# An attention and deformable-convolution block: five turns per tile moved from TensorE to DRAM blocks and VectorE, row biases moved into accumulating DMAs, orders replanned

## The chip, the cores and the metric

The kernel runs on one core of one Trainium2 chip. The metric is the device time of one execution in microseconds (us). Several executions are timed and their median is given; one more execution is recorded by the hardware profiler, and all busy times, waits and durations come from that one.

The core has TensorE (PE, with its weight loads shown as PEld), VectorE (DVE), ScalarE (ACT), GpSimd (POOL) and SyncE (SP). SP computes nothing here. It issues DMAs, each after the waits that stand ahead of it in SP's own order.

## The reference

Two layers on an image batch `x` of shape (4, 64, 64, 256), all in float32.

```
# layer 0: self-attention over the 4096 pixels of each image
q, k, v = x @ wq + bq, x @ wk + bk, x @ wv + bv          # q, k: 32 channels, v: 256
x = gamma * softmax(q k^T) v + x

# layer 1: deformable convolution (16 groups of 16 channels, 9 points), then an MLP
h      = ln(x) * ln1_g + ln1_b
proj   = h @ inproj_w + inproj_b                         # padded by one pixel
c      = gelu(ln(depthwise3x3(h) + dw_b))
offset = c @ off_w + off_b                               # (x, y) of 16 * 9 points
mask   = softmax over the 9 points of (c @ mask_w + mask_b)
s      = sum over the points of mask * bilinear(proj at the pixel + point + offset)
x      = x + s @ outproj_w + outproj_b
h      = ln(x) * ln2_g + ln2_b
x      = x + gelu(h @ fc1_w + fc1_b) @ fc2_w + fc2_b
```

## The kernel before

The 16384 pixels are cut into 64 tiles of 256 (UN = 64; NU = 16 tiles for each of the 4 images, 128 pixels twice on the partitions). A tile passes through these stages, each a dictionary of named steps:

- `project(b, u)` turns a tile of x, so that its channels lie on the partitions, and makes keys, queries (`keys`, `key_bias`) and values. For image 0 this comes ahead of everything (the stage "first", turned on TensorE). For the images 1 to 3 it is done while the image before is in attention; there x is read in blocks of 32x32 by `in_blocks` (four DMAs of 128-byte pieces, which put each block where its turned form belongs), and one VectorE transpose (`copy`, L645) turns the values inside each block. Keys, queries and values of later images go through DRAM (`kd`, `qd`, `vd`).
- `Attention` makes the energies `e` (L752), their exponentials `ex` on ScalarE (L762) and the weighted sums `acc` (L774), with a column of ones for the softmax's denominator.
- `front` adds the attention's result times gamma to x (`inverse`, `residual`), takes the statistics, normalises (`norm`), turns (`turn`), scales, puts the result into a strip of image rows `hs` (`image`), adds outproj_b to x and stores it as `x1d` (`keep`), and projects it and stores the padded image `xp` (`project_in`, `store`).
- `plan(v)` works on tiles that are shifted by half a tile (65 of them, the first and last half as long): the nine taps of the depthwise convolution on `cv` (L874, L878), a turn (`turn`, tile `pc`, L891), layer norm, a turn back (`turn2`, `pt_p`), gelu, the heads for offsets and masks (`po`, L915), and from these the weights `wn` of a 5x5 window around each pixel.
- `sample(v)` loads five shifted rows of `xp` (`win`, L1074), multiplies them by the weights (`times`, L1094) and adds them up (`plus`, L1102; `across`), giving `sp`.
- `back(v)` (built by `finish`) turns sp (`pt_s`), applies outproj, adds it to x1 (`added`, L1182), layer norm, a turn (`pt_b`), fc1 in eight parts `ph` (L1200), gelu (L1208), fc2 (`pmlp`, L1217), and stores the result (`end`, L1223). `raised` (L1189) adds fc2_b.

So a tile is turned on TensorE five times after the attention: `pt_f`, `pc`, `pt_p`, `pt_s`, `pt_b`. Such a turn is four matmuls against the identity matrix `ident` (`transposed`, L331, for four of the five). It writes PSUM, and ScalarE or VectorE takes it from there. The row biases bv, inproj_b, outproj_b and fc2_b are added by VectorE, each with one operation on 128x512 elements (L681, L838, L824, L1189), from copies that all partitions hold.

Layer norm's `1/sqrt` is done on GpSimd (`rstd`: L289 adds epsilon, L290 takes the power), between VectorE's statistics (`mv`, L287) and VectorE's `nm` (L295), the shift that ScalarE's `norm` needs.

The order in which each engine does its work is written out: the table `WHEN` has a time for every step within a slot of T = 60 units, the table `LATE` has other times for the last slots (from 59 on), and `whole` sorts all steps of all tiles by slot and time. Only the order counts, and each engine follows it. Slot s holds the attention of tile s and, further on in the pipeline, `front`, `plan`, `sample` and `back` of earlier tiles. DMAs take SP's queue in the order of the steps that issue them.

A further part of the program (a loop over `whole(True)`, and rounds for points outside the 5x5 window) runs only if the data ask for it. One such round for far points, `far_round`, is always run at the end.

## Time and profile before

| | |
|---|---|
| median of 3 runs | 3754.59 us (3753.15 to 3758.33) |
| the profiled execution's own time | 3755.45 us |
| its span, first to last instruction | 3753.7 us, mean granted TensorE clock 0.995 |
| PE, PEld | 98%, 85% of the span busy |
| DVE, ACT, POOL | 92%, 57%, 8% busy |
| DMA queue of SP | 51.9% of the 16 engines' span, 508 MB |
| DMA issues of SP with most calls | win<-xp 536, kT<-kd 512, qs<-qd 256, xs<-in_x_dram 192 |

A busy share is an average over the whole run. Matmuls are pipelined, and their recorded durations overlap; the cost of a matmul in a row of them is the distance from its start to the start of the next. The same holds for VectorE's operations, which overlap by some 0.08 us.

### The profile page before, as it was taken

To read this page: it belongs to the slowest core of one execution; us is meant where nothing else is said; L and a number is where in the kernel's file an instruction comes from. 1 tells how busy PE (TensorE), PEld (TensorE's weight loads), DVE (VectorE), ACT (ScalarE), POOL (GpSimd) and SP (SyncE) were. 2 spreads that over 40 slices of the span, in tenths; PEclk is the share of its full clock that TensorE was granted. 3 is DMA by queue.
4 is the path that set the end of the run, shared out by engine and by line. 5 is a ranking of instruction groups with operands and counts; after the bars stand their busy time and mean duration, and the time that the engine had idled before them with its cause. 6 is when DMAs were issued, how large, how long until landed. Compare 5 with 4: busy or idle time off the path is not lost.

```text
span 3753.7 us, 53218 instructions
## 1 busy us (share of the span) xinstructions
PE 3693.6 (98%) x18226; PEld 3185.1 (85%) x18226; DVE 3442.1 (92%) x6307; ACT 2122.0 (57%) x4085; POOL 313.1 (8%) x444
## 2 busy tenths in 40 slices
PE   7999999999999999999999999999999999999988
PEld 6888888888888888888888888888888888888867
DVE  2499999999999999999999999999999999999995
ACT  2465565565565565565565555555565665565543
POOL 1000000000000000000000000000000000000021
PEclk9999999999999999999999999999999999999999
DMA  6555545556555555555656455555565545544531
GB/s 185 142 130 140 143 129 140 141 129 175 149 149 146 138 131 143 134 135 143 176 137 164 129 138 142 129 139 140 138 174 146 136 124 136 132 129 126 135 83 52
DMA packets 370088, 518.42 MB, mean 138 GB/s; under 512 B 144560, under 2 KB 287472, under 8 KB 369808
## 3 DMA queue, kind: packets, MB, share of 16 engines
q1 hardware_dynamic: 359904, 508.02, 51.9%
q10 hardware_dynamic: 8320, 3.43, 0.4%
q8 instruction: 147, 2.41, 0.3%
q0 software_dynamic: 1584, 3.47, 0.3%
q14 instruction: 133, 1.09, 0.1%
HBM read 385.91 MB, written 128.85 MB: 137 GB/s over the span
## 4 chain that ended last, share of the span: by engine, by line
PE 89%; DVE 5%; issue 0%; DMA 0%; ACT 0%; POOL 0%; DVEq 0%; SPq 0%; ACTq 0%; POOLq 0%
PE acc L774 43%; PE pmlp L1217 11%; PE ph L1200 11%; PE e L752 6%; PE po L915 5%; PE pout L1175 3%; PE pp L831 3%; PE pv L670 2%; DVE pw L1094 1%; PE pkq L651 1%; DVE cv L878 1%; DVE pw L1102 1%; PE pt_s L331 1%; PE pt_b L331 1%; PE pt_p L331 1%; PE pc L891 1%
## 5 line engine op out<-in xcount | busy, mean ns | idle before, releaser
L774 PE MATMUL acc<-V,ex 128*128 128x257 f32 x8192 | 1887.0, 380 | 0.0
L774 PEld LDWEIGHTS acc<-V,ex 128*128 128x128 f32 x8192 | 1537.3, 190 | 223.3 <-issue 21.7
L1094 DVE TENSOR_TENSOR pw<-win,wn 128x1280 f32<-128x1280 f32 x640 | 931.5, 1481 | 10.9 <-ACT wn L1038 1.9
L1102 DVE TENSOR_TENSOR pw<-pw,pw 128x1280 f32<-128x1280 f32 x492 | 729.7, 1483 | 0.1
L762 ACT ACTIVATE ex<-e 128x512 f32<-128x512 f32 x1024 | 529.7, 605 | 26.1 <-PE e L752 18.0
L1200 PE MATMUL ph<-hT_b,f1w 128*128 128x256 f32 (+1 forms) x2080 | 487.9, 377 | 5.2 <-ACT gT L1208 2.8
L1217 PE MATMUL pmlp<-f2w,gT 128*128 128x256 f32 x2048 | 462.7, 379 | 1.3 <-DVE x1b L1182 1.1
L1200 PEld LDWEIGHTS ph<-hT_b,f1w 128*128 128x128 f32 x2080 | 378.1, 190 | 67.3 <-ACT gT L1208 6.3
L1217 PEld LDWEIGHTS pmlp<-f2w,gT 128*128 128x128 f32 x2048 | 384.2, 190 | 51.8 <-DVE x1b L1182 1.4
L878 DVE SCALAR_TENSOR_TENSOR cv<-hs,dw,cv 128x256 f32<-128x256 f32 (+1 forms) x1076 | 424.3, 459 | 1.4 <-ACT cv L874 1.3
L303 ACT ACTIVATE xn_p<-pc,nm_p,rstd_p 128x256 f32<-128x256 f32 x128 | 65.4, 561 | 541.1 <-DVE nm_p L295 541.1
L1208 ACT ACTIVATE gT<-ph,f1b 128x256 f32<-128x256 f32 (+1 forms) x520 | 236.6, 468 | 236.1 <-PE ph L1200 234.6
L752 PE MATMUL e<-qs,kT 128*128 128x256 f32 x2048 | 321.7, 300 | 0.0
L752 PEld LDWEIGHTS e<-qs,kT 128*128 128x128 f32 x2048 | 271.4, 190 | 8.1 <-ACT ex L762 0.8
L762 ACT ACT_TABLE_LOAD x182 | 233.5, 1283 | 3.1
L289 POOL TENSOR_SCALAR rstd_p<-mv_p 128x2 f32<-128x2 f32 (+1 forms) x65 | 76.2, 1172 | 1669.1 <-DVE mv_p L287 1597.9
L915 PE MATMUL po<-om_w,ge 128*128 128x432 f32 x512 | 196.5, 526 | 0.8 <-ACT ge L908 0.8
L1004 DVE TENSOR_TENSOR pr<-hat 128x1296 f32<-128x1296 f32 x128 | 192.6, 1505 | 0.0
L1208 ACT ACT_TABLE_LOAD x124 | 159.1, 1283 | 2.2
L915 PEld LDWEIGHTS po<-om_w,ge 128*128 128x128 f32 x512 | 96.9, 190 | 70.5 <-issue 54.7
L908 ACT ACTIVATE ge<-pt_p,bd,gd 128x256 f32<-128x256 f32 (+1 forms) x130 | 66.0, 558 | 137.9 <-PE pt_p L331 137.9
L303 ACT ACTIVATE xn_b<-x1b,nm_b,rstd_b 128x256 f32<-128x256 f32 x128 | 70.0, 593 | 129.8 <-DVE nm_b L295 129.8
(220 smaller groups left out, 3823.0 us busy)
## 6 DMA issues: line engine op xcount, KB each, us to landing
win<-xp SPq DMA_DIRECT2D x536, 320.0 KB, 4.5
kT<-kd SPq DMA_DIRECT2D x512, 256.0 KB, 4.2
omd<-om SPq DMA_DIRECT2D x63, 432.0 KB, 2.6
x<-in_x_dram SPq DMA_DIRECT2D x64, 256.0 KB, 3.0
x1d<-x SPq DMA_DIRECT2D x64, 256.0 KB, 2.2
xp<-xq SPq DMA_DIRECT2D x128, 128.0 KB, 2.4
x1b<-x1d SPq DMA_DIRECT2D x63, 256.0 KB, 3.2
spd<-sp SPq DMA_DIRECT2D x63, 256.0 KB, 2.2
```

Of the source, the lines that this page charges most:

```text
L303: nc.scalar.activation(xn[:, i, :], s, AF.Identity, bias=nm[:, i : i + 1], scale=st["r"][:, i : i + 1])
L752: nc.tensor.matmul(es[r][:, jj, :], lhsT=self.kT[g][:, 4 * jj + r, :], rhs=self.qs.bitcast(F32R), start=True, stop=not self.general,)
L762: nc.scalar.activation(ex, self.es[r], AF.Exp)
L774: nc.tensor.matmul(self.acc[i], lhsT=ex[:, jj, i * P : (i + 1) * P], rhs=V[t // 2][:, t % 2, :], start=(g == 0 and r == 0 and jj == 0), st ...
L878: nc.vector.scalar_tensor_tensor(dst, src, dw[:, k, j : j + 1], dst, ALU.mult, ALU.add)
L915: nc.tensor.matmul(st["po", i], lhsT=st["ge"][:, k, i * P : (i + 1) * P], rhs=om_w[:, k, :], start=(k == 0), stop=(k == 1),)
L1004: nc.vector.tensor_mul(pr.rearrange("p a b c d g -> p a b (c d g)"), hat[:, :, i, 1, :].unsqueeze(1).to_broadcast([P, 3, 3, S]), hat[:, :, ...
L1094: nc.vector.tensor_mul(st[r].rearrange("p d (g c) -> p (d g) c", c=GC), src.rearrange("p d (g c) -> p (d g) c", c=GC), wns[v][:, i, r] .re ...
L1102: nc.vector.tensor_add(st[0], st[0], st[r])
L1200: nc.tensor.matmul(ph[:, :m], lhsT=f1w[:, k, c * P : (c + 1) * P], rhs=st["hT"][:, k, :m], start=(k == 0), stop=(k == 1),)
L1208: nc.scalar.activation(st["gT"][:, c, :m], st["ph", c][:, :m], AF.Gelu, bias=f1b[:, c : c + 1])
L1217: nc.tensor.matmul(po, lhsT=st["gT"][:, c, i * P : (i + 1) * P], rhs=f2w[:, c, :], start=(c == 0), stop=(c == NH - 1),)
```

## The change

The five turns of a tile leave TensorE for most tiles. A tile that is to be turned is written to DRAM by SP (`sent`, into one of four buffers `ways`), read back in blocks of 32x32 by the four DMAs of `in_blocks` (`blocks`), and turned inside the blocks by one VectorE transpose (`swapped`). For sp the copy that was written to DRAM anyway (`spd`) serves. The first tile and the last four to seven keep the turns on TensorE: each stage has a condition of the form `0 < v < UN - 5`. The condition is on the tile's number, UN - 4 for the turn in `front`, UN - 5 for both in `plan`, UN - 6 for both in `back`.

The row biases leave VectorE. ScalarE writes gamma*bv into the tile of x ahead of time (`base`), and x is then added by an accumulating DMA of GpSimd (`input`); the values are scaled by gamma instead. The same is done with outproj_b (`base` and `load` in `back`). SP fills the image `xp` and the output in DRAM with inproj_b and fc2_b (`fill`), and an accumulating DMA of GpSimd adds the tile (`store`). Some VectorE work is merged (two sums, two mask products, two reciprocals), and the inner hat goes to ScalarE.

All orders are new: `WHEN` has other numbers for every stage, and `LATE` now covers the first slots (0 to 4, and the stage "first") and the slots from 55 on. The numbers of both tables are left out below.

```diff
+    ways = dram.tile([4, 256, C], F32, name="ways")
+    turns = [0]
+
+    def blocks(name, src=None, read=None):
+        t = p1.tile([P, 2, 256], F32, tag="xs", bufs=2, name=f"bl_{name}")
+        in_blocks(t, *(read or (src, 0, 2)))
+        return t
+
+    def sent(src):
+        way = ways[turns[0] % 4]
+        turns[0] += 1
+        nc.sync.dma_start(way.rearrange("(q p) c -> p q c", p=P), src)
+        return way
+
+    def swapped(dst, bl):
+        nc.vector.transpose(dst.rearrange("p k t -> p (k t)"), bl.rearrange("p k t -> p (k t)"))
+        return dst
...
-        def value_bias():
-            bias = bv_s.unsqueeze(1).to_broadcast([P, 2, C])
...
-                nc.vector.tensor_add(vs, st["pv"], bias)
+                nc.scalar.activation(vs, st["pv"], AF.Identity, scale=gamma_s)
...
+        def base(self):
             self.x = p2.tile([P, 2, C], F32, tag="x1", name=f"x1_{self.n}")
-            nc.sync.dma_start(self.x, xt_[self.b, self.u])
+            nc.scalar.copy(self.x, gbv.unsqueeze(1).to_broadcast([P, 2, C]))
+
+        def input(self):
+            nc.gpsimd.dma_start(self.x, xt_[self.b, self.u], accum_op=ALU.add)
...
+        through = 0 < b * NU + u < (UN if att.general else UN - 4)
...
             normalised(st, [att.x[:, i, :] for i in range(2)], f"f{n}")
+            if through:
+                st["way"] = sent(st["xn"])
 
         def turn():
-            st["pt"] = transposed(st["xn"], f"f_{n}")
+            if through:
+                st["bl"] = blocks(f"f_{n}", st["way"])
+            else:
+                st["pt"] = transposed(st["xn"], f"f_{n}")
+
+        def swap():
+            st["hT"] = swapped(p3.tile([P, C // P, 256], F32, tag="cT", name=f"hT_f{n}"), st["bl"])
...
+        def fill():
+            nc.sync.dma_start(
+                xp[b, 2 + 4 * u : 6 + 4 * u, 2 : 2 + W, :],
+                bass.AP(inproj_b.tensor, inproj_b.offset, [[0, 4], [0, W], [1, C]]),
+            )
+
+        def take():
+            st["xq"] = p1.tile([P, 2, C], F32, tag="xq", name=f"xq_{n}")
+            nc.scalar.copy(st["xq"], st["pp"])
+
         def store():
-            xq = p1.tile([P, 2, C], F32, tag="xq", name=f"xq_{n}")
-            nc.vector.tensor_add(xq, st["pp"], inb.unsqueeze(1).to_broadcast([P, 2, C]))
             for r in range(2):
-                nc.sync.dma_start(
+                nc.gpsimd.dma_start(
                     xp[b, 2 + 4 * u : 6 + 4 * u, 2 : 2 + W, :].rearrange("(q r) w c -> r w q c", r=2)[r],
-                    xq[r * W : (r + 1) * W, :, :],
+                    st["xq"][r * W : (r + 1) * W, :, :], accum_op=ALU.add,
                 )
...
+        through = 0 < v < (UN if general else UN - 5)
+
         def turn():
+            if through:
+                st["bl"] = blocks(f"c_{n}", sent(st["cv"]))
+                return
...
-            nc.vector.scalar_tensor_tensor(
-                hat[:, 1], hat[:, 0], 1.0, hat[:, 2], ALU.subtract, ALU.subtract, reverse0=True
-            )
+            nc.scalar.activation(hat[:, 1], xy, AF.Abs)
+            nc.scalar.activation(hat[:, 1], hat[:, 1], AF.Identity, bias=every[:, 0:1], scale=-1.0)
...
-    def back(v, sps):
+    def back(v, sps, general):
...
+        def base():
+            st["x1"] = p2.tile([P, 2, C], F32, tag="x1b", name=f"x1b_{v}")[:, :nt]
+            nc.scalar.copy(st["x1"], ob.unsqueeze(1).to_broadcast([P, nt, C]))
+
         def load():
-            st["x1"] = p2.tile([P, 2, C], F32, tag="x1b", name=f"x1b_{v}")[:, :nt]
-            nc.sync.dma_start(st["x1"], x1t_[:, g0 : g0 + nt])
+            nc.gpsimd.dma_start(st["x1"], x1t_[:, g0 : g0 + nt], accum_op=ALU.add)
+
+        def fill():
+            nc.sync.dma_start(
+                outs[g0 * P : (g0 + nt) * P, :],
+                bass.AP(fc2_b.tensor, fc2_b.offset, [[0, nt * P], [1, C]]),
+            )
+
+        def store():
+            nc.gpsimd.dma_start(out_[:, g0 : g0 + nt], st["x1"], accum_op=ALU.add)
```

## The prediction

> **What bounds the kernel now.** I read section 1 of the page and the chain first, then the windows by stage, then the timeline of one steady slot on TensorE and VectorE.
>
> ```profile
> PE 3693.6 (98%) x18226; PEld 3185.1 (85%) x18226; DVE 3442.1 (92%) x6307; ACT 2122.0 (57%) x4085; POOL 313.1 (8%) x444
> PE 89%; DVE 5%; issue 0%; DMA 0%; ACT 0%; POOL 0%; DVEq 0%; SPq 0%; ACTq 0%; POOLq 0%
> ```
>
> ```profile
> 60.00:150.00 90.00, 85.56 (x421) 73.74 (x420) 23.84 (x63) 44.67 (x80) 1.76 (x4) 0.98 0.59 143
> 2000.00:3000.00 1000.00, 1000.00 (x4968) 866.66 (x4967) 957.11 (x1721) 587.57 (x1125) 79.04 (x108) 1.00 0.55 143
> 3500.00:3600.00 100.00, 94.56 (x453) 79.00 (x451) 99.47 (x183) 46.78 (x92) 9.94 (x13) 1.00 0.38 100
> ```
>
> Columns of the windows: stretch, length, busy PE, PEld, DVE, ACT, POOL, granted clock, DMA share, GB/s. From about 150 to 3400 us PE never pauses, so there PE's work is the time; DVE follows at 96%. PE loses 23 us before 150 us and 29 us after 3400 (one window of that stretch is shown). A slot of the loop, read between two turns of sp:
>
> ```profile
> 2001.51 0.60 PE L331 MATMUL pt_s<-ident,sp 128*128 128x128 f32 x4
> 2001.86 1.19 PE L752 MATMUL e<-qs,kT 128*128 128x256 f32 x8
> ...
> 2022.45 0.60 PE L331 MATMUL pt_f<-ident,xn_f 128*128 128x128 f32 x4
> 2022.88 1.90 PE L774 MATMUL acc<-V,ex 128*128 128x257 f32 x8
> ...
> 2057.99 0.60 PE L331 MATMUL pt_s<-ident,sp 128*128 128x128 f32 x4
> ```
>
> From 2001.51 to 2057.99 is 56.48 us. Matmuls overlap, so a turn costs what lies between its start and the next start: 0.35 (pt_s), 0.43 (pt_f), and on the same timeline 0.44 (pc), 0.43 (pt_p), 0.36 (pt_b). In the same slot DVE's pauses are these, 2.54 us in all, so its work is 53.9 us:
>
> ```profile
> 2004.82 0.69 DVE L1182 TENSOR_TENSOR x1b<-x1b,pout 128x512 f32<-128x512 f32 x1 [0.16 <-PE pout L1175]
> 2009.25 0.16 DVE L295 SCALAR_TENSOR_TENSOR nm_b<-mv_b,rstd_b 128x2 f32<-128x2 f32 x1 [0.60 <-POOL rstd_b L290]
> 2011.75 0.17 DVE L797 RECIPROCAL rall<-acc 128x1 f32<-128x1 f32 x1 [0.23 <-PE acc L774]
> 2044.36 0.69 DVE L1223 TENSOR_TENSOR x1b<-x1b,pmlp 128x512 f32<-128x512 f32 x1 [0.85 <-PE pmlp L1217]
> 2053.27 0.61 DVE L924 TENSOR_TENSOR om<-po,om_b 128x432 f32<-128x432 f32 x1 [0.70 <-PE po L915]
> ```
>
> **What the Trainium skill says.** "VectorE: DVE Perf Modes", The three transpose paths: VectorE turns only 32x32 blocks; the placing of the blocks is left to the block reads. The trace has this already for x: one STREAM_TRANSPOSE of 128x512 takes 703 ns. "DMA: Bandwidth & Descriptors", Two DMAs through the same engine are not ordered: a read of what another DMA wrote must wait for the first one's completion. So each turn now pays a whole write and then a read: 2.0 us (vd<-vs) and 2.6 us (xs<-in_x_dram) to landing in this trace. The same page, SWDGE vs HWDGE: accumulation during a DMA can only be issued from GpSimd; no run here shows an accumulating DMA yet. "SBUF — State Buffer", SBUF: two separate sides: a GpSimd op that reads SBUF can be locked out by a running DVE op with two SBUF inputs. The trace agrees: L289 for rstd_p, started beside a 1.48 us pw<-win, has a median of 1291 ns, for rstd_b 327 ns.
>
> **The change part by part, in us per slot of 56.48.**
>
> PE: five turns go, 0.35+0.43+0.44+0.43+0.36 = 2.01. Nothing is added, so PE needs 54.47. By the limits in the code, pt_f goes in 59 slots, pc and pt_p in 58, pt_s and pt_b in 57: 59x0.43 + 58x0.87 + 57x0.71 = 116 us in all. This is the most that the removal can give.
>
> DVE: five block transposes at 0.63 from start to start (703 ns less the 0.08 by which neighbours overlap): +3.14. Removed, in the same measure: f2b 0.60, ob 0.57, inb 0.60, bv 0.60, inner hat 0.61, two products with gamma 0.17, one reciprocal 0.08, and by merging two mask products and two sums 0.07+0.16: -3.46. Net -0.3, so 53.6 of work. In the last batch (slots from 48 on) the bv add is absent anyway, and DVE gains 0.3 of work.
>
> DVE's new waits, from the built order and these durations. (a) After mv_p DVE runs a 1.40 us plus and two 0.10 us bounds before nm_p needs rstd_p. L289 is locked out until the plus ends; then L290 takes 0.71: about 0.7 of wait. (b) On SP the reads for swap of hT_b stand behind the stores of kq, and these wait for kq1 (L659). From there: two issues 0.8, three reads at 0.69, the last landing 2.6: 5.5 us; DVE has 4.6 us of work between. Wait (a) lies in the same stretch, so both together cost about 1.0. Bounds: 0 (SP runs ahead) and 2.5 (each landing 1.5 longer). (c) The pauses for po, pmlp and pout now come at other places; in the order they come after DVE's waits have let PE run ahead, so I take 0, at most the old 1.7. Sum for DVE 54.6, beside PE's 54.5: nearly equal. I take 54.7 a slot. What is late next is then DVE, and PE waits for its block transposes.
>
> ACT: copies of gbv and ob, the scaling of vs and the copy of xq at 0.59 each (the row sT<-pt_s), Abs and Identity at 0.67 each (the row hat<-om), less the copy sT: +3.1 on 33.2. Cover: ACT is idle 23 us per slot. Nothing on the path.
>
> SP: 20 more block reads at 0.69, three sends and two fills at about 0.45; less x, x1b, out and two xp (2.9): +13.2 us of issuing. SP's waits are some 36 us of a slot, so the total fits; the order of its waits decides, as in (b). The two writes of image and result wait for their fills, which stand half a slot ahead of them: 0.
>
> POOL: five accumulating DMAs per slot. Their issue is not in the trace: from 0.59 (xp<-zeros) to 1.45 (indirect f_am), so 3 to 7 us beside 5 of work. Behind a waiting one stand L289 and L290 of rstd_p, and behind these DVE's nm_p. The store of xq is the one just ahead; it waits for ACT's copy of pp, which PE finishes some 2 us before mv_p. I take 0; bounds 0 and 1.5. A gain is excluded, since a wait is only added.
>
> DMA share: 55% now. 289 block reads of 256 KB in 128-byte pieces: 2048 pieces at 13 ns (the mean of such packets in the trace) on 16 engines, 1.66 us each, 13% of the span. Sends (174 of 256 pieces of 1 KB at 58 ns, likewise) 4%, fills 3%; accumulation at between one and three times a plain transfer, 0 to 12%. Sum 75 to 87%. Not the bound, but landings may lengthen; that is the upper end of (b).
>
> Head and tail: all orders of slots 0 to 4 and 55 on are new, and the last turns stay on PE. PE idles 52 us there. I take a gain of 5, bounds +35 (8.3 us pass before the first x lands, and I leave 9 for the last serial steps) and -20.
>
> Sum against the profiled run (3755.45, span 3753.7): slots 2 to 47, 46 x 1.8 = 83; ten slots of the last batch, where PE would fall from 53.9 to 51.9 but DVE with its waits holds at 53.4: 5; ends 5. 3755.45 - 93 = 3662; the median of the runs is 0.9 below the profiled run: 3661, forecast **3660**.
>
> **Rivals.**
> 1. DVE becomes the bound by a clear margin: waits (a), (b) and POOL sum to 2 us rather than 1. The slot is 55.6, the gain 46 x 0.9 = 41, nothing in the last batch: 3710 (3690 to 3745). For it: the balance of 54.6 to 54.5. Against: DVE idles 2.5 us per slot today, and the order puts other work between.
> 2. The way through DRAM is late: a turn takes 0.1 + 2.0 + 0.1 + 3x0.69 + 2.6 = 6.9 us on an SP queue in which a late send also holds back win and kT. Place: SP's sends and reads, waited for by DVE at the block transposes. It decides from about 1.9 us per slot beyond the 1.0 of (b), where the gain of PE is used up. At 3.5 us beyond, the slot is 58: 3755 + 56x1.5 = 3840, **slower**. For it: SP's load grows by two thirds and DMA goes to about 80%. Against: every pair of send and swap that I placed has 8 to 12 us of DVE work between.
> 3. The ends: with the full 116 and 35 at the ends it would be 3755 - 151 = 3604; 20 lost there with the likeliest rest gives 3685.
> 4. The turns don't leave PE (the limits exclude most slots): excluded, since the built order has no turn on PE in the slots between.
>
> **The numbers.** About 0.2% is what a measurement of this kernel can tell from no change: 7.5 us. Likeliest case 0.57, 3660 (3625 to 3690); rival 1 0.22; rival 2 0.14; a result within 0.2% 0.03; ends at their best 0.04. Faster 0.83, same 0.03, slower 0.14. The range from 3600 to 3780 leaves out most of rival 2 and little below.
>
> **What would show it.** Right: PE has no L331 rows in mid-run, is busy 98% or more from 300 to 2900 us, and a slot is 54.5 to 55. Step (a) is right if DVE waits some 0.7 us per slot for POOL's rstd_p; (b) if it waits under 1 us for bl_b. The DMA step is wrong if block reads need over 4 us to land, POOL's if rstd_p waits for xq. The forecast is wrong if PE's busy share falls below 96% in mid-run, with waits for the block transposes (rival 1, then 2).

## The result, and the profile after

The changed kernel takes **4341.91 us** (median of 4 runs, 4330.33 to 4347.3) beside 3754.36 for the kernel before: a ratio of 1.1559 (1.1534 to 1.1584). It is 588 us slower; 3660 was forecast, with 0.14 on slower. Its profiled execution took 4330.33 us (span 4328.4), at a mean TensorE clock of 0.942, where before had 0.995.

Section 1 of the page after, and its chain:

```profile
PE 3791.3 (88%) x17070; PEld 3180.7 (73%) x17070; DVE 3493.9 (81%) x5974; ACT 2208.9 (51%) x4306; POOL 694.4 (16%) x766
DVE 39%; DMA 29%; SPq 11%; PE 8%; ACT 5%; issue 5%; POOL 1%; DVEq 0%; ACTq 0%; POOLq 0%
```

The 1156 matmuls of the turns are gone (x18226 to x17070), as planned. But nothing is the bound any more: PE and DVE both have holes, and the chain, which was 89% PE, is now 40% DMA and SP's queue. The same three windows after:

```profile
60.00:150.00 90.00, 79.44 (x385) 68.86 (x384) 16.57 (x43) 39.36 (x70) 4.18 (x5) 0.96 0.57 133
2000.00:3000.00 1000.00, 875.50 (x3919) 737.06 (x3918) 827.83 (x1388) 509.51 (x1001) 151.43 (x166) 0.94 0.76 166
3500.00:3600.00 100.00, 88.80 (x388) 72.72 (x387) 84.52 (x140) 49.09 (x98) 12.47 (x14) 0.93 0.76 168
```

In mid-run PE does 3919 matmuls in 1000 us, where it did 4968, and it idles 124.5 us. A slot, read from one start of `pr` to the same one of the next tile, is 66.4 us in slots 16 to 32 and 65.7 in slots 32 to 48 (56.5 and 56.2 before). The first `pr` starts 34 us later, what follows the last is 21 us longer, and the last four slots gain 18 us: of the 575 us between the two profiled executions the ends cost 37 and the slots 538.

The slot splits in two. From 1000 to 3000 us, some 30 slots of 66.4 us, PE is busy 1750.7 us, or 58.1 us a slot, and idle 8.3. So 8.3 us of a slot are waits, and 3.6 are PE's own work of 54.5 taking 58.1. The waits of PE, then of DVE, in this stretch (total us, times, longest):

```profile
PE ph L1838 <- ACT hT_b L335: 170.6, 30, 10.6
PE po L1544 <- ACT ge L1537: 59.0, 30, 6.1
```

```profile
DVE ge L296 <- DMA bl_p<-ways: 103.2, 28, 6.0
DVE pc L296 <- DMA bl_c<-ways: 65.2, 29, 3.0
DVE kq L1252 <- ACT kq L1251: 59.4, 27, 6.3
DVE hT_b L296 <- DMA bl_b<-ways: 36.0, 28, 6.5
DVE nm_p L315 <- POOL rstd_p L310: 21.4, 30, 0.7
```

PE waits for the two tiles that come out of turned blocks, `hT_b` and `ge`; ACT, which scales them, waits for DVE's transpose; DVE waits for the block reads. These three block waits are 6.8 us a slot. Line by line on SP's timeline (start, duration, engine, line, operation), this is how the blocks for `ge` come late:

```profile
2012.36 0.69 SPq L1437 DMA_DIRECT2D xp<-in_L_conv_inproj_b_dram  x1
2015.56 0.38 SPq L292 DMA_DIRECT2D ways<-cv  x1
...
2023.56 2.78 SPq L76 DMA_DIRECT2D bl_c<-ways  x4
...
2034.84 0.38 SPq L292 DMA_DIRECT2D ways<-pc  x1
2035.27 1.11 SPq L1701 DMA_DIRECT2D win<-xp  x2
2036.48 1.19 SPq L1310 DMA_DIRECT2D kT<-kd  x2
2037.72 4.71 SPq L1701 DMA_DIRECT2D win<-xp  x4
2042.47 2.63 SPq L76 DMA_DIRECT2D bl_p<-ways  x4
```

```profile
2050.57 0.71 DVE L296 STREAM_TRANSPOSE ge<-bl_p 128x512 f32<-128x512 f32 x1 [2.97 <-DMA bl_p<-ways]
```

`pc` is sent at 2034.84. Its reads stand behind eight other DMAs on SP and start 7.6 us later; the transpose runs 15.7 us after the send. The reads also land later than the 2.6 us that the prediction took: from the last issue to the transpose pass some 6 us here, and 6.4 in the median of the 28 slots in which DVE waits for them, with the DMA engines full (a share of 1.02 from 2036 to 2050.5 us). The send of `cv` goes out just behind a fill, and its reads start 8.0 us after it. SP waits for `ways<-cv` 28 times in these 2000 us, 7.9 us at worst. The late landing of this send acts on a second way too. ACT's `far` is written into the buffer of `cv` and waits for the send, 81.8 us in 28 waits; ACT's `kq` comes next, and DVE's 59.4 us of waits for `kq` follow. In e1_noacc (below), which has no fills, DVE waits 0.6 us for `bl_c` and nowhere for `kq`, ACT waits 1.2 for the send, and PE's wait for `hT_b` is 23.0 us instead of 170.6.

What the pauses then do to PE, on its timeline after:

```profile
2036.29 9.30 PE L1838 MATMUL ph<-hT_b,f1w 128*128 128x256 f32 x32 [6.00 <-ACT hT_b L335]
```

Thirty-two matmuls take 9.30 us after 6.00 us of idleness. In the run without fills (e1_noacc, below) 32 of the same kind took 7.23 us after 1.35. The clock that the trace records is 0.5 from 2033.8 to 2040.6 us and 1.0 after that. From 1000 to 3000 us it is 0.5 for 8.4 us of a slot; PE works in 6.3 of these and so loses 3.1 us, most of the 3.6.

### The profile page after: what moved, and what is told of

The parts are those of the page before. It is cut to its first block, busy times and chain, and to the rows that moved or that the text cites. A ratio compares the mean times of both kernels' runs of the same rounds, so it can differ in the third digit from the quotient of the medians.

```text
span 4328.4 us, 52964 instructions
## 1 busy us (share of the span) xinstructions
PE 3791.3 (88%) x17070; PEld 3180.7 (73%) x17070; DVE 3493.9 (81%) x5974; ACT 2208.9 (51%) x4306; POOL 694.4 (16%) x766
## 4 chain that ended last, share of the span: by engine, by line
DVE 39%; DMA 29%; SPq 11%; PE 8%; ACT 5%; issue 5%; POOL 1%; DVEq 0%; ACTq 0%; POOLq 0%
DMA ways<-cv 9%; SPq L76 8%; DVE pw L1719 8%; DVE pw L1727 7%; DVE cv L1489 7%; DMA bl_p<-ways 4%; PE acc L1369 4%; DVE pr L1630 3%; DMA bl_b<-ways 3%; DMA kT<-kd 2%; DMA spd<-sp 2%; DMA win<-xp 2%; DVE om L1553 1%; DMA bl_s<-spd 1%; DMA bl_x<-in_x_dram 1%
## 5 line engine op out<-in xcount | busy, mean ns | idle before, releaser
L1369 PE MATMUL acc<-V,ex 128*128 128x257 f32 x8192 | 1851.0, 381 | 12.6 <-ACT ex L1359 8.9
L1838 PE MATMUL ph<-hT_b,f1w 128*128 128x256 f32 (+1 forms) x2080 | 589.7, 448 | 299.4 <-ACT hT_b L335 288.1
L1838 PEld LDWEIGHTS ph<-hT_b,f1w 128*128 128x128 f32 x2080 | 458.4, 231 | 413.5 <-ACT hT_b L335 303.0
L1544 PE MATMUL po<-om_w,ge 128*128 128x432 f32 x512 | 249.8, 640 | 120.7 <-ACT ge L1537 120.7
L1349 PE MATMUL e<-qs,kT 128*128 128x256 f32 x2048 | 339.3, 307 | 16.8 <-ACT ex L1359 8.6
L1891 POOL DMA_DIRECT2D x1b<-x1d x65 | 82.6, 1271 | 1401.7 <-ACT x1b L1888 1351.9
L1644 ACT COPY us<-pr 128x144 f32<-128x144 f32 x128 | 40.4, 316 | 325.8 <-DVE pr L1630 325.6
L1571 ACT ACTIVATE hat<-om 128x576 f32<-128x576 f32 (+1 forms) x130 | 86.9, 669 | 221.3 <-DVE om L1553 221.3
L296 DVE STREAM_TRANSPOSE ge<-bl_p 128x512 f32<-128x512 f32 x58 | 41.2, 711 | 194.4 <-DMA bl_p<-ways 194.4
L1537 ACT ACTIVATE ge<-ge,bd,gd 128x256 f32<-128x256 f32 x116 | 63.3, 593 | 229.5 <-DVE ge L296 229.5
```

What stands on the lines that cost most here:

```text
L1349: nc.tensor.matmul(es[r][:, jj, :], lhsT=self.kT[g][:, 4 * jj + r, :], rhs=self.qs.bitcast(F32R), start=True, stop=not self.general,)
L1369: nc.tensor.matmul(self.acc[:, i, : C + 1], lhsT=ex[:, jj, i * P : (i + 1) * P], rhs=V[t // 2][:, t % 2, :], start=(g == 0 and r == 0 and ...
L1544: nc.tensor.matmul(st["po", i], lhsT=st["ge"][:, k, i * P : (i + 1) * P], rhs=om_w[:, k, :], start=(k == 0), stop=(k == 1),)
L1838: nc.tensor.matmul(ph[:, :m], lhsT=f1w[:, k, c * P : (c + 1) * P], rhs=st["hT"][:, k, :m], start=(k == 0), stop=(k == 1),)
```

## The experiments

One thing first, which the text ahead of the prediction tells too simply. The orders written out are those of PE, DVE, ACT and POOL. SP's order follows from them and from durations that a planner assumes when the program is built. So an edit can move SP's DMAs, and several runs below differ in that too. The expectations also put a slot at 64.6 us for after and 61.1 for e1_noacc; by the starts of `pr` from 1000 to 3000 us these are 66.4 and 62.3.

### One part at a time

**e1_noacc**: turns and orders stay; the fills go, and POOL's DMAs are plain ones. The row biases are left out.

```diff
-            nc.gpsimd.dma_start(self.x, xt_[self.b, self.u], accum_op=ALU.add)
+            nc.gpsimd.dma_start(self.x, xt_[self.b, self.u])
...   (likewise load and both stores; base no longer copies gbv and ob)
         def fill():
-            nc.sync.dma_start(...)
+            pass
```

> The changed kernel with its turns through DRAM and its orders as they are, but without the two fills per slot and with the five GpSimd DMAs per slot plain instead of accumulating (same queue, same bytes). Left out of the computation: the additions of the four row biases bv, inproj_b, outproj_b and fc2_b, which are zero in this input. TensorE, VectorE and ScalarE have the work of the changed kernel (ScalarE 1.2 us less per slot). T1 (fills and accumulating DMAs clog the rings, so that the sends land late: ways<-cv took about 8 us in the slot looked at, 2 were assumed): ways<-cv lands in about 3 us, the slot falls from 64.6 to 56 us or less, time 3700 to 3850. T2 (the way through DRAM itself is late: block reads of 128-byte pieces and SP's single queue of 13 us more issuing): slot stays above 61 us, time 4150 to 4300. T3 (the new orders alone): 4250 to 4340.

Measured: 4124.31 us, ratio 1.0978 (1.0960 to 1.0996). So 218 us belong to fills and accumulation (ScalarE's two copies, 1.2 us a slot, go with them), and 370 remain. PE's waits from 1000 to 3000 us:

```profile
PE po L1540 <- ACT ge L1533: 143.8, 32, 7.8
PE ph L1834 <- ACT hT_b L335: 23.0, 15, 6.3
```

These two are 166.8 of PE's 176.0 us of idleness there, and behind them DVE waits 126.9 us for `bl_p` and 37.2 for `bl_b`.

**e1_peturns** and **e1_orders**: in slots 5 to 52 the turns go back to PE, just ahead of their use, with fills and accumulation (e1_peturns) and without (e1_orders).

```diff
         def swap2():
+            if ppe:
+                return
             st["pt"] = swapped(p3.tile(...), st["bl"])
...
         def gelu():
+            if ppe:
+                st["pt"] = transposed(st["xn"], f"p_{n}", nt)
...   (likewise the other four; far has a tile of its own)
```

> The changed kernel with its fills, accumulating DMAs and orders, but in slots 5 to 52 the five turns are made on TensorE again, each just ahead of its consumer (2 us of TensorE more per slot; ScalarE copies sT again; pc is read from PSUM). So no sends and only the block reads of x on SP, and VectorE is rid of five block transposes (3.1 us). T1: fills and accumulation still hold back kT and win, but nothing turns in series through them; the slot is 58 to 61, time 3900 to 4050. T2: the slot is 56.5 to 57.5, time 3760 to 3830. T3: still above 62 us a slot, time above 4150.

> Both at once: turns on TensorE in slots 5 to 52, no fills, plain GpSimd DMAs; only the new orders, the plain GpSimd queue and the work moved from VectorE to ScalarE remain of the change. Left out: the additions of the four row biases, zero in this input. T1 and T2 both expect a TensorE-bound slot of 56.5 us and 3740 to 3800. T3 (the orders, planned for other durations, are at fault): above 4100.

Measured: 4289.3 us, 1.1420 (1.1401 to 1.1439), and 4177.73 us, 1.1129 (1.1110 to 1.1147). These miss their aim. The turns take their places in two PSUM buffers that are used in turn, and `pt_s` stands there behind the tile of `pmlp`: PE waits for DVE's `end` 124.2 us in 31 slots of the first and 128.7 in the second. They say nothing on what the orders cost; e5_floor answers that.

**e1_fill64**: the fill of `xp` is laid out as 64 pieces of 4 instead of 4 of 64.

```diff
-                xp[b, 2 + 4 * u : 6 + 4 * u, 2 : 2 + W, :],
-                bass.AP(inproj_b.tensor, inproj_b.offset, [[0, 4], [0, W], [1, C]]),
+                xp[b, 2 + 4 * u : 6 + 4 * u, 2 : 2 + W, :].rearrange("r w c -> w r c"),
+                bass.AP(inproj_b.tensor, inproj_b.offset, [[0, W], [0, 4], [1, C]]),
```

> Only the access pattern of the image's fill changes: 64 outer rows of 4 instead of 4 outer rows of 64 (same 256 pieces of 1 KB). The planner of SP's order then issues the fills far ahead, about three slots' worth in each of the slots up to about 28, and none after that; all else is the changed kernel. T1: the second half runs as if there were no fills: if the fills are the greater part, its slot is under 59 us and ways<-cv lands in 3 us; if the accumulation is, it stays at 62 or more. Time 4000 to 4250. T2 and T3: both halves at 64 us, time 4280 to 4350.

Measured: 4486.47 us, 1.1943 (1.1923 to 1.1963), worse than after. The Trainium skill, "DMA: Bandwidth & Descriptors", Rules for kernel authors, says that a DMA whose outermost size is 4 is confined to at most four engines. The packets of after agree: a stretch of such a fill moves 35 to 39 pieces of 1 KB in half a microsecond at 50 to 72 ns each, about four to five engines' time. Spread over all, though, the pieces themselves become slow. All pieces of a fill are read from one row in DRAM; 16,899 pieces of 1 KB of SP's queue took over 150 ns here, 5473 in after and 646 in e1_noacc. That the fills also came in bunches here may have its part in it: the planner issued some three slots' fills in each slot, until the last at 1639 us. By accident this tells a second thing. From 1000 to 2000 us PE does 3533 matmuls; the next 1000 us are without fills:

```profile
2000.00:3000.00 1000.00, 910.00 (x4161) 765.21 (x4160) 874.51 (x1468) 537.96 (x1057) 160.60 (x176) 0.96 0.76 167
```

With all accumulation PE does 4161 matmuls in this stretch; e1_noacc, without either, does 4150. So **accumulating costs no time that shows here; the fills do**. SP's order differs between these two runs; e3_hand_rows, below, holds it.

**e2_rows**: the fills are read from 256 rows in DRAM that hold the same bias; the outermost size for `xp` is still 4.

```diff
-                bass.AP(inproj_b.tensor, inproj_b.offset, [[0, 4], [0, W], [1, C]]),
+                rows_b[0].rearrange("(r w) c -> r w c", w=W),
```

> The changed kernel with one edit: each fill copies 256 rows of 1 KB that lie apart in DRAM (the bias written out 256 times ahead) instead of one row of 1 KB read 256 times. Pieces, destinations and the place on SP stay. In the run with the reshaped fill 36 pieces of 1 KB started per 0.5 us while fills ran, against 178 beside other transfers[...]. F1 (the one source row is what makes a fill slow): the fills run at the rate of other 1 KB pieces, ways<-cv lands in about 3 us, and the time comes near that of the kernel without fills and accumulation: 4120 to 4180. F2 (the image's fill is slow because of its 4 outer rows): only the fill of the result gets faster, 4220 to 4290. F3 (it is the accumulating DMAs): 4310 to 4350.

Measured: 4287.54 us, 1.1394 (1.1363 to 1.1425). Slow pieces fall to 1220, but only 54 us come back. `pc`'s transpose then waits for other DMAs ahead of it on SP (`kT` 46.2 us, `bl_c` 34.3, `qd` 17.3), and `bl_p` still for 122.8.

### Can the trips be sent earlier?

All four start from e1_noacc, without row biases.

**e2_early**: the reads for `ge` and `hT_b` are due some 8 units earlier.

```diff
-            ... "turn2": 32.6415, ...     (plan)
+            ... "turn2": 24.5, ...
-            ... "turn2": 79.8113, ...     (back)
+            ... "turn2": 71.0, ...
```

> The kernel without fills and accumulation (row biases left out), with two numbers of the order changed, the due times of the block reads of p (32.6 to 24.5) and of b (79.8 to 71.0), so that SP issues bl_p two places behind ways<-pc instead of behind eight loads of win and kT, and bl_b ahead of the stores of kq. There VectorE waited 4.0 us per slot for bl_p and 1.2 for bl_b, and these were nearly all of TensorE's 5.4 us of idleness per slot. A (what stands ahead of the block reads on SP and in its rings makes them late): the waits fall below 1 us, slot 56 to 57.5 against 61.1, time 3830 to 3930. B (128-byte block reads land late wherever they stand): waits about halve, 3980 to 4060. C (neither, the orders of the engines): 4100 to 4130.

Measured: 4151.2 us, 1.1046 (1.1028 to 1.1065): no gain. DVE's waits:

```profile
DVE hT_f L296 <- DMA bl_f<-ways: 178.0, 30, 7.3
...
DVE ge L296 <- DMA bl_p<-ways: 9.3, 2, 6.4
```

The wait for `bl_p` is gone, and `bl_f`, which had none to speak of (12.1), has more than `bl_p` ever had: it now stands on SP behind `spd<-sp`, which waits for DVE. What the place on SP does to a read shows here too. `bl_p` is issued two DMAs behind its send where eight stood between, and each of its reads lands sooner (issue to landing from 1000 to 3000 us, first in e1_noacc, then in e2_early):

```profile
DMA to landing us min/median/max: 5.7/7.3/10.8
DMA to landing us min/median/max: 2.3/2.5/4.3
```

So the loads ahead of it made the read not only start late but land late.

**e2_actq**: sends and reads of four turns are issued from ACT.

```diff
-        nc.sync.dma_start(way.rearrange("(q p) c -> p q c", p=P), src)
+        nc.scalar.dma_start(way.rearrange("(q p) c -> p q c", p=P), src)
...   (likewise in_blocks for bl_f, bl_c, bl_p, bl_b; bl_c is due at 14.3, bl_b at 76.0)
```

> The kernel without fills and accumulation (row biases left out), with the four sends and their block reads issued from ScalarE's queue in place of SP's (the reads of x and of sp stay on SP; the due times of bl_c and bl_b are set so that ScalarE doesn't wait long for a landing). SP is rid of 14 us of issuing per slot, and a turn no longer stands in the rings behind win and kT. ScalarE gets about 12 us more of issuing. A: as in the run with early reads or better, slot 55.5 to 57, time 3780 to 3900, if ScalarE's waits for landings cost nothing. B: block reads still land late, 3980 to 4100. C: 4100 or more.

Measured: 4439.78 us, 1.1826 (1.1804 to 1.1847). ACT stands still for a send's landing before it can issue the reads, issuing four takes it 2.6 us or more, and what it should compute meanwhile is late: DVE waits 218.2 us for ACT's `kq`.

**e2_pb**: `pt_p` and `pt_b` stay on PE in slots 5 to 52, the other three go through DRAM.

```diff
+    PET = 'pb'
...   (these two are made by transposed in slots 5 to 52, as in e1_peturns)
```

> The kernel without fills and accumulation (row biases left out), with the turns of p and b back on TensorE in slots 5 to 52 (0.8 us of TensorE more per slot, two block transposes of VectorE less); f, c and s stay on the way through DRAM. A and B: the two late turns are gone and the other three have slack, slot 55.5 to 57, time 3770 to 3880, so that most of the loss lies in these two turns. C (the orders of the engines cost it): above 4050.

Measured: 4158.62 us, 1.1063 (1.1045 to 1.1082). The waits for `bl_p` and `bl_b` are gone with the trips, and `bl_f` takes over once more (184.4 us in 27 waits), with 89.0 for `pt_b`.

**e3_hand**: SP's order is written out too, with the reads as early as I thought their sends allowed.

```diff
-        with tc.manual_schedule(engines={nc.tensor.engine, nc.vector.engine, nc.scalar.engine, nc.gpsimd.engine}):
+        with tc.manual_schedule(engines={..., nc.gpsimd.engine, nc.sync.engine}):
...
+            "turn": -17.0,   (front)   "read": 12.0, "turn2": 28.0,   (plan)   "turn2": 72.5,   (back)
```

> The kernel without fills and accumulation (row biases left out), with SP's order no longer left to the planner but taken from the due times like those of the other engines, and the due times of four block reads moved up: bl_c 12.0 (apart from its send at 9.2), bl_b 72.5, bl_p 28.0, bl_f -17.0. In the two runs with bl_p and bl_b mended VectorE waited 5.7 to 6.8 us per slot for bl_f instead, which the planner had put behind spd<-sp, a store that waits for VectorE. A (the place of each read in SP's one queue makes it late, now this one, now that): no read stands behind such a wait, waits for block reads below 1.5 us per slot in all, slot 55.5 to 57.5, time 3770 to 3900. D (the orders of VectorE and TensorE leave a turn too little time wherever its read stands): another wait takes the place again, slot above 60, time 4050 to 4150.

Measured: 4369.02 us, 1.1628 (1.1609 to 1.1648). My order is worse than the planner's: the loads of the queries, which stand just ahead of their use, now stand behind sends that wait (`ways<-cv` 197.2 us for DVE's `cv`, in 30 slots). PE's first wait:

```profile
PE e L1348 <- DMA qs<-qd: 246.9, 30, 11.3
```

**e3_hand_rows** adds accumulation and fills to e3_hand, with 64 outermost and distinct rows; **e3_hand_fills** adds both as after has them. SP's hand-written order is the same in the three.

```diff
+                xp[b, 2 + 4 * u : 6 + 4 * u, 2 : 2 + W, :].rearrange("r w c -> w r c"),
+                rows_b[0].rearrange("(r w) c -> w r c", w=W),
```

> As the run with SP's order by hand, but with fills and accumulating DMAs as in the changed kernel and all biases computed; the fills copy from 256 rows apart and with 64 outer rows. In the changed kernel the two fills cost 3.6 us per slot (64.6 against 61.0 in the stretch without fills). If each fill now runs at the rate of other pieces of 1 KB, two fills take about 2 us of the rings' time and cost under 1 us per slot beside the run by hand without them: 20 to 60 us more than it. If fills are slow because they go from DRAM to DRAM, the cost stays near 3.6 us per slot: 150 to 230 us more.

> The changed kernel as it is, fills, accumulation and biases, with SP's order by hand and the four due times as in the run by hand. A: 4342 falls by the same 250 to 350 us as without fills: 3990 to 4100. D: 4270 to 4350.

Measured: 4402.16 us, 1.1722 (1.1702 to 1.1742), and 4573.26 us, 1.2181 (1.2161 to 1.2202). With SP's order held, fills and accumulation cost 33 us when spread over engines and rows, and 204 as the change has them. This is the cleanest test of the fills, though it changes their shape and their source together.

### Without a trip at all

**e4_short**: VectorE transposes the tile in SBUF; every send and read is still made, and nobody waits for it. So a tile is turned inside its blocks only.

```diff
-            st["hT"] = swapped(p3.tile(...), st["bl"])
+            st["hT"] = swapped(p3.tile(...), st["xn"])
...   (likewise pc, ge, sT and hT_b; far has a tile of its own)
```

> The changed kernel with all its sends and block reads, but nobody reads what the block reads bring: VectorE's five block transposes take the tile in SBUF that was sent (for b the sum x1b), so they wait for no DMA. far has a tile of its own. Left out is the placing of the blocks, so the values are not the reference's. All DMA traffic, SP's issuing, fills and accumulation and the orders of the other engines stay. If the trips' lateness as such is the cause (rival 2 of the prediction): slot 54.7 to 57, time 3660 to 3850. If the orders of TensorE and VectorE are at fault apart from the trips, or the traffic through other loads (kT, win, qs): above 4100.

**e4_short_nodma**: the same without the sends and block reads. **e5_floor**: the same without fills and accumulation too, as in e1_noacc.

```diff
     def blocks(name, src=None, read=None):
+        if name[0] != "x":
+            return None
...
-        nc.sync.dma_start(way.rearrange("(q p) c -> p q c", p=P), src)
         return way
```

> As the run before it, and the sends and the block reads of f, c, p, s and b are not issued either; fills and accumulation stay. Against the run before it this gives what SP's 13 us of issuing and 17% of the DMA engines' time cost beside the trips: 0 to 40 us if they are covered, as the prediction had it, over 150 if kT, win and qs are held back. It is also the floor of the changed kernel with turns that are free of any trip: the prediction's 54.7 us a slot gives 3660. If it stays above 4000, the orders themselves are slow.

> The changed kernel's orders with nothing of the new DMA work: turns free of any trip (no sends, no block reads, VectorE turns what lies in SBUF, so the values aren't the reference's), no fills, plain instead of accumulating DMAs, row biases left out. Extra rounds for far points, which the wrong values bring, add about 97 us at the end (the tail after the last pr was 172 us in both runs with such turns, 73 in the changed kernel). If the prediction's sum per slot was right apart from the trips and fills: slot 54.7, 3660 + 97 = 3757. If the new orders by themselves cost something: slot 56 or more, 3840 or more.

Measured: 4345.97 us, 1.1563 (1.1546 to 1.1581); 4048.67, 1.0774 (1.0757 to 1.0790); 3910.94, 1.0417 (1.0402 to 1.0433). The values that come of this send more points out of the 5x5 window, and two more rounds for far points run at the end: after the last `pr` there are 170.5, 172.1 and 172.6 us, where after has 72.6. Less that difference they are 4248, 3949 and 3811. With this correction:

| us | no fills, no accumulation | both |
|---|---|---|
| turns cost DVE's transpose alone | 3811 (e5_floor) | 3949 (e4_short_nodma) |
| turns through DRAM | 4124 (e1_noacc) | 4342 (after) |

Before has 3754. So orders and merged work alone cost 57, where 93 were to be gained; trips add 313 to 393, fills and accumulation 138 to 218. SP's order is the planner's in all four, and `far` has a tile of its own in the two without trips, so these differences hold that too. By the starts of `pr`, 12 of the 57 us lie in slots 2 to 48, 34 in slots 48 to 60, and the rest at the two ends. In e5_floor, PE's waits from 1000 to 3000 us are no longer behind a block read:

```profile
PE po L1541 <- ACT ge L1534: 59.7, 33, 8.4
PE ph L1835 <- ACT hT_b L336: 13.4, 31, 1.3
```

A slot there is 56.7 us: PE's 54.6 of work and 2.1 of these waits. DVE is busy 54.2.

e4_short held a surprise. With nobody waiting for a trip it is still 299 us over e4_short_nodma. PE's first wait there:

```profile
PE e L1349 <- DMA qs<-qd: 212.1, 30, 12.5
```

So sends and reads hurt also as DMAs that others queue behind. But the planner had arranged SP anew, and how much of the 299 is its order and how much the full queue was not separated.

### One trip alone, in the kernel before

**e4_before_f**: the kernel before, with the turn of `front` alone sent through DRAM, for tiles 1 to 56. The two DMA steps stand where SP's order suggested (19.12 and 22.0), the transpose at 28.5.

```diff
+            "sent": 19.12, "read": 22.0, "swap": 28.5,
...
+                nc.sync.dma_start(ways[slot % 2].rearrange("(q p) c -> p q c", p=P), st["xn"])
...
+                in_blocks(st["bl"], ways[slot % 2], 0, 2)
...
+                nc.vector.transpose(st["hT"].rearrange(...), st["bl"].rearrange(...))
```

> The kernel before with one turn alone through DRAM: xn_f is sent behind norm (19.1), its blocks are read at 22.0 into the idle buffer of xq, and VectorE turns them at 28.5, just ahead of where TensorE did at 29.2; slots 1 to 56, no other order changed, biases where they were. In the order before there are 10 us between norm and turn of f. TensorE 0.43 less per slot, VectorE 0.63 more (53.9 to 54.5 of 56). If a trip is harmless where the order leaves it 10 us: 56 x 0.43 = 24 less at most, 3730 to 3745. If any turn through DRAM makes VectorE or SP late: above 3770.

Measured: 4140.61 us, 1.1024 (1.1009 to 1.1039). **A single trip per tile, with no fill and no other step moved, costs 384 us.** Its timeline shows the whole way:

```profile
2047.11 0.15 DVE L297 SCALAR_TENSOR_TENSOR nm_f<-mv_f,rstd_f 128x2 f32<-128x2 f32 x1
...
2049.32 1.08 ACT L305 ACTIVATE xn_f<-x,nm_f,rstd_f 128x256 f32<-128x256 f32 x2
...
2050.43 0.38 SPq L821 DMA_DIRECT2D ways<-xn_f  x1
...
2053.53 2.60 SPq L76 DMA_DIRECT2D bl_f<-ways  x4
...
2058.36 0.71 DVE L831 STREAM_TRANSPOSE hT_f<-bl_f 128x512 f32<-128x512 f32 x1 [6.27 <-DMA bl_f<-ways]
```

From DVE's `nm_f` to DVE's transpose pass 11.2 us (10.6 in the median of 31 slots): 2.2 until ACT comes to it, 1.1 for ACT's work, 3.1 from the send's start until the reads start (they wait for its landing, and two reads of `xs` stand between), 2.6 to issue the four and 2.2 to the last landing. DVE has about 4.9 us of work in between and waits 6.27.

**e5_before_f2**: shift, norm and send come earlier and the transpose later, so that DVE has 11.1 us of work in between.

```diff
-            "shift": 9.44, "norm": 19.11, ... "sent": 19.12, "read": 22.0, "swap": 28.5, "scale": 30.3, "project_in": 34.83, "store": 36.13,
+            "shift": 8.6, "norm": 8.65, ... "sent": 8.66, "read": 10.0, "swap": 34.6, "scale": 34.62, "project_in": 37.0, "store": 38.24,
```

> The kernel before with the turn of f through DRAM, as in the run before, but with more of VectorE's work put between nm_f and the block transpose: shift and norm of f earlier (9.44 to 8.6, 19.1 to 8.65), swap at 34.6, scale 34.62, project_in 37.0, store 38.24. In the run before, 4.9 us of VectorE's work lay between them, the trip took 11.2 us from nm_f, and VectorE waited the missing 6 us in each slot. Now 11.1 us lie between. If the loss of a trip is just its length less the work ordered between, VectorE waits under 0.7 us per slot and the time is 3735 to 3775. If a late turn costs as such (SP's queue, the in-order engines), it stays near 4100.

Measured: 4120.87 us, 1.0981 (1.0966 to 1.0996). DVE's wait for `bl_f` is gone (1.4 us in all), and the time is not. PE's wait, and what it does to the matmuls behind it, with the same matmuls of before as the last line:

```profile
PE pp L857 <- ACT hT_f L842: 139.9, 32, 4.8
```

```profile
2048.16 3.78 PE L857 MATMUL pp<-inw,hT_f 128*128 128x256 f32 x8 [4.30 <-ACT hT_f L842]
```

```profile
2024.62 1.89 PE L831 MATMUL pp<-inw,hT_f 128*128 128x256 f32 x8
```

DVE's transpose comes late in DVE's order, and PE's `pp` came too early in PE's for it.

**e6_before_f3** puts `pp` later as well (39.3, its store 40.5, and `value_bias` 38.24). **e7_control** is that order with the turn on PE.

```diff
-            ... "value_bias": 42.74, ...   (project)   ... "project_in": 37.0, ... "store": 38.24,   (front)
+            ... "value_bias": 38.24, ...   (project)   ... "project_in": 39.3, ... "store": 40.5,   (front)
```

> The kernel before with the turn of f through DRAM and swap at 34.6 as in the last run, and the work that hangs on hT_f put later on TensorE too: project_in from 37.0 to 39.3 (behind values and two groups of acc, 5.4 us of TensorE's work), store from 38.24 to 40.5, value_bias from 42.74 to 38.24. In the last run VectorE no longer waited for bl_f (1.4 us in 32 slots), but TensorE waited 4.4 us per slot at pp for hT_f, and the matmuls behind that pause ran slower (eight of pp took 3.8 us). If the trip costs only where some engine's order has too little work for its whole length, TensorE now has that work, waits under 1 us, and the time is 3730 to 3800. If a trip in this chain closes a loop over the slots that no order of one engine can open, the wait goes to the next member (st_p for pc, win or ge) and the time stays above 3950.

> The kernel before with the order of the last run (shift, norm, scale, project_in, store and value_bias moved as there), but the turn of f left on TensorE, just ahead of scale. It parts what is left in the last run, 3812 against 3756 or 0.8 us per slot: if that is the moved order, this kernel takes 3790 to 3830 as well; if it is the trip (SP holding win behind the landing, VectorE's 0.63 us of block transpose), this kernel takes 3750 to 3765.

Measured: 3812.14 us, 1.0150 (1.0136 to 1.0164), and 3763.17 us, 1.0023 (1.0014 to 1.0031). Of e6_before_f3, PE's waits from 1000 to 3000 us:

```profile
PE po L941 <- DVE kq L661: 14.4, 8, 5.4
PE ph L1226 <- DVE vs L683: 12.5, 31, 0.8
PE pp L857 <- ACT hT_f L842: 1.7, 5, 0.7
```

Moving three steps in the orders of PE and DVE wins 309 us over e5_before_f2. But the trip that is placed well costs 49 us against the same order with the turn on PE; the 56 turns that it spares are 0.43 us each, 24 us. No kernel tried is faster than before.

## Why the prediction was wrong, point by point

**The step that failed** is the one against rival 2: "every pair of send and swap that I placed has 8 to 12 us of DVE work between", set beside a trip of 6.9 us. The work between was there: after has 8.5 us (sp) to 12.2 us (`ge`) of it in the median from 1000 to 3000 us. The trip was mis-sized, and the count was made on one engine alone.
- The trip was too short in the sum. Alone, at a DMA share of 0.52, it takes 11.2 us from `nm_f` in the slot shown, or 7.9 from the send. There the two landings were close to what I took (2.2 to 3.8 and 2.3 to 3.2 us in e4_before_f, where 2.0 and 2.6 stood); what lacked were ACT's turn and ACT's work ahead of the send, and what stands between on SP.
- SP is an engine in its own order. I counted the work between on DVE, and never counted what stands between send and read on SP. For `bl_p` that is eight DMAs and 7.6 us, and behind them its reads take some 6 us to land, so the trip is 15.7. The prediction's own sign, reads that need over 4 us to land, came true for this read (7.3 us in e1_noacc, and 2.5 in e2_early, which issues it ahead of the loads). The sends were miscounted as well: four a slot and 232 in all, not three and 174.
- PE has an order too. e5_before_f2 has its 11.1 us of DVE work and still loses 366 us, because `pp` stood where the old turn had allowed it.

**(b)**, about 1.0 us with bounds of 0 and 2.5, looked at one of five reads. For that one, `bl_b`, DVE waits 1.2 us a slot, so the size was near. The three that are waited for cost 6.8 us of DVE's time a slot, and PE's waits behind them 7.6. Rival 2 was the right mechanism, but with 3.5 us beyond (b) it was priced at 58 us a slot, where the slot is 66; and 0.14 was too little for a case whose decisive number, SP's order, I could have read in the built order.

**PE 54.47** was right as work: e5_floor has 54.6. But the sum holds PE's work fixed while it waits. After pauses, PE is slower: 58.1 us a slot. The Trainium skill, "TensorE: Matmul & The Clock Gate", Part 1: The HAM clock gate, states that an idle window of some 3.4 us halves the clock, until it has been busy for as long. The traces agree: the eight `pp` of e5_before_f2 take 3.78 us after 4.30 us of idleness, and 1.89 in before, and the clock that they record is 0.5 over such stretches (2047.1 to 2053.9 us there). In after this is 3.1 of the 3.6 us that PE's work takes longer in a slot, about a third of the loss of 10 us, and the prediction had no term for it.

**The fills**: "stand half a slot ahead: 0". Nobody waits for a fill, as I said. But a fill stands ahead of a send in the same queue, and this was not priced: with accumulation 138 us without trips, 218 with them. DVE's wait for `bl_c`, which is read behind that send, is 65.2 us in after and 0.6 in e1_noacc, and the wait for `kq`, late by way of ACT's `far`, is 59.4 and none. The cause is the fills' shape and source together (33 against 204 us with SP's order held); the new shape alone gave 145 us more, the new source alone 54 less.

**DVE 53.6** and the slot of **54.7**: DVE is busy 54.2 us in e5_floor, and the slot is 56.7. One of the new waits was put at nothing: ACT's Abs and Identity stand in DVE's chain for the hat, and `am` waits 0.5 us a slot for them (14.9 us in 29 waits after, 18.2 in 35 in e5_floor, where `rstd_p` makes DVE wait 25.2 and `win` 21.1). Even with free turns, then, no gain was left.

**Right** were (a), 0.7 us for `rstd_p` (21.4 us in 30 waits); (c), since DVE's old pauses for `po`, `pmlp` and `pout` are gone; POOL, whose issues take up to 1.28 us (`x1b<-x1d`) and hold `rstd_p` back nowhere from 1000 to 3000 us; and accumulation, which costs no time that shows. The DMA share, 76% in 75 to 87, was right by luck: of a slot of 66.4 us it is 50 us, where 75 to 87% of 54.7 is 41 to 48.

**The ends**: 5 us of gain were taken, or 20 of loss at worst; 37 were lost.

**What stays open**: the trips' 313 us are SP's order, its full queue and PE's clock together. In each of the four tries something else became late, and no order was found that keeps all five reads early, so how much a good order would recover is not known. Why the well-placed trip still costs 49 us was not tested. DVE's own transposes, 0.63 us for each of 56 tiles, are 35, in a slot where DVE was 96% busy.

## What to carry to other kernels

When an operation on the bound engine is replaced by a way through DRAM, price the way as a latency from the last input's producer to the consumer, and compare it with what stands between these two in the order of *every* engine on the way, the DMA queue's own first; the smallest of them counts. Add what a pause does to the bound engine afterwards: each gap of over 4 us in PE also slowed the matmuls that followed here. Nor is a landing time a constant: the same read took 7.3 us behind eight large loads and 2.5 ahead of them. And a transfer that nobody waits for can still be the one that others queue behind, so look at its shape (the outermost size) and its source (one row, or many).

## What the runs showed of the hardware that I had not expected

- Reading one DRAM row many times is slow: of SP's pieces of 1 KB, 5473 took over 150 ns in after, 1220 when the same fills came from 256 rows (e2_rows) and 646 without fills (e1_noacc); the typical piece takes 46 ns. With the fills from one row laid out as 64 pieces of 4 it was 16,899, though there they also came in bunches.
- An accumulating piece of 1 KB takes 102 ns in the median, about double a plain one (46), and had no cost in time at a DMA share of 0.76.
- SP's issues can stretch: four `win<-xp` took 4.71 us in after, where two took 1.11 just before. That the queue was full by then is likely and not shown.
- A pause of 4.3 us in PE makes the next eight matmuls take double the time, so a wait costs more than its own length: in e4_before_f 4.8 us of waits a slot came with 5.3 us at a clock of 0.5, in which PE worked 4.5 and lost 2.2. Pauses of 0.6 to 1.8 us did not do this: after each of 17 such pauses ahead of `po` in after, the first eight matmuls took 376 ns each from start to start, and 653 to 720 after four pauses of 4.7 to 6.1 us; after 2.1 to 2.9 us both 376 and some 587 occur.
